# A scheduler's rank with a margin for small products: one term and one earliest time in a list-scheduled feed-forward kernel

## The chip, the cores and the metric

The kernel runs on one core of a Trainium2 chip. The metric is the time of one execution in microseconds (us). Before the change four executions took 459.94, 460.02, 460.11 and 460.18 us, median 460.06 us. The profile page was taken from one execution of 459.97 us.

## The reference

The input x is 64 samples of 64 channels by 1024 time steps. Each sample has a condition number, which picks a 64x64 matrix. The channels are mixed with it, and the result passes a linear layer with a gated low-rank addition (8 experts of rank 16, the best two of each token weighted by a softmax). The input is added at the end.

```python
W = weights[condition]                                   # 64 of 16 matrices, 64x64
h = jnp.einsum('bct,bcd->bdt', x, W)                     # condition mixing
gate_logits = jnp.einsum('bsd,ed->bse', h, gate_w)
weights, selected = jax.lax.top_k(gate_logits, 2)        # softmax over the two
result = jnp.einsum('bsd,od->bso', h, base_w) + base_b
low = jnp.einsum('bsd,erd->ebsr', h, lora_A)
lora_out = jnp.einsum('ebsr,eor,bse->bso', low, lora_B, w_full)
return x + result + 2.0 * lora_out
```

All is float32. The order of the two linear steps can be exchanged, and the kernel does that: it multiplies x by the wide weights first and applies the condition matrix to the product.

## The kernel before

**Tiling.** Tokens go in 32 tiles of 128 (two samples each). The weights of low-rank part, gate and base layer are put side by side and cut into three column blocks of 384, 388 and 388 columns; the 1024 inputs are cut into four pairs of 128. To keep float32 accuracy each operand is split into a high part (a rounded copy, made by ScalarE or VectorE, names `xh`, `wh_...`, `zh`, `bdh`, `lth`) and a low part (the difference, made by VectorE, names `xl`, `wl_...`, `zl`, `bdl`, `ltl`). Every product is then three matmuls: high by high, high by low, low by high (`zstep`, L407).

**Stages.** The first two pairs of tiles (`PLAIN`) are multiplied plainly while the weights arrive and are split. The other 14 pairs use a scheme with fewer products: sums of x blocks (`sum_x`, L292) and sums of weight blocks (`mix_w`, L342) are multiplied in a fixed order (`HEAD`, `TAIL`, `FINAL`), and the products are added and subtracted on VectorE into `st` buffers (`mix`, L740). A finished column block (`chunk`) is split (`split_z`) and goes to `post`.

**Small products.** `post` applies the condition matrix: `sums` (L434, matmuls on L447) multiplies `zh`, `zl` with `bdh`, `bdl`, and later adds the low-rank part with `lth`, `ltl`; `gate` works on the gate's logits; `tr` (L497, matmul on L500) transposes the weighted low-rank part. These steps of TensorE are marked `first=True`, except in the last two tiles. The big products are chained by the name `"order"`, so they keep their order; the small ones may stand anywhere between them.

**Condition matrices.** `load_cond` (L391) gathers one 128x128 matrix by an indirect DMA of GpSimd into `bdr`, casts it on ScalarE to `bdh` and subtracts on VectorE to `bdl`. There are two buffers. The first two loads stand at L597 and L598.

**The order of the work** is made at build time. `Program.add` records steps, each with its engines and the planner's assumed costs, what it reads and writes, and a due time. `Program.run` (L111) then lists them. It first goes backwards and gives each step a rank `late`: the latest start that keeps all due times, by the assumed costs. Then it goes forwards: it takes the engine that can start soonest, and on it, of the steps that are ready by then, one marked `first` if there is one, else the one of the smallest `late`. A step marked `first` is only offered `MARGIN` (1.2) after its inputs, so that on the chip it should not have to wait. `after=` gives a step an earliest time in the planner's own clock, and `early=True` keeps a step from being listed more than `AHEAD` (10) before its `late`. What comes out is a fixed order of instructions for TensorE, VectorE, ScalarE, GpSimd and the DMA queue of SyncE; on the chip an engine's instructions run in that order, each waiting for its inputs.

```python
for i in reversed(range(n)):
    s = steps[i]
    c, e = min(s["eng"].values()), next(iter(s["eng"]))
    late[i] = min([s["due"] - c] + [late[j] - hop(e, next(iter(steps[j]["eng"]))) - s["lag"] - c
                                    for j in succ[i]])
...
i, r = min(((i, r) for i, r in cand[e] if (max(r, port) if steps[i]["port"] else r) <= t + 1e-9),
           key=lambda q: (not steps[q[0]]["first"], late[q[0]], q[0]))
```

Of the kernel before, what the change touches and what calls it, by code (L numbers as in the profile page):

```python
# [41 lines left out]
PE, ACT, DVE, POOL, SP = "PE", "ACT", "DVE", "POOL", "SP"  # L42
# [4 lines left out]
ISSUE = 0.45  # L47
FLIGHT, DMA = 2.0, 1 / 360e3
QUEUE = 3.0
FIRST = 11.0  # L50
TWICE = 2.5
AHEAD = 10.0
MARGIN = 1.2
# [26 lines left out]
class Program:  # L80
# [7 lines left out]
    def add(self, engine, cost, fn, reads=(), writes=(), due=None, first=False, size=0.0, early=None, port=False,  # L88
            after=0.0):

        n = len(self.steps)
        engine, cost = (e if isinstance(e, (list, tuple)) else [e] for e in (engine, cost))
        deps = set()
        for b in list(reads) + list(writes):
            if b in self.writer:
                deps.add(self.writer[b])
        for b in writes:
            deps.update(self.readers.get(b, ()))  # L100
        for b in reads:
            self.readers.setdefault(b, []).append(n)
        for b in writes:
            self.writer[b], self.readers[b] = n, []
        deps.discard(n)
        self.steps.append(dict(eng=dict(zip(engine, cost)), fn=fn, deps=deps, first=first, size=size, port=port,
                               lag=FLIGHT + QUEUE + size * DMA if size else 0.0, after=after,
                               due=self.horizon if due is None else due,
                               early=SP in engine and not reads if early is None else early))

    def run(self):  # L111
        steps, n = self.steps, len(self.steps)
        succ = [[] for _ in steps]
        for i, s in enumerate(steps):
            for d in s["deps"]:
                succ[d].append(i)
        hop = lambda a, b: SAME[a] if a == b else HOP[a]
        late = [0.0] * n
        for i in reversed(range(n)):
            s = steps[i]  # L120
            c, e = min(s["eng"].values()), next(iter(s["eng"]))
            late[i] = min([s["due"] - c] + [late[j] - hop(e, next(iter(steps[j]["eng"]))) - s["lag"] - c
                                            for j in succ[i]])
        left = [len(s["deps"]) for s in steps]
        ready, end, by = [0.0] * n, [0.0] * n, [None] * n
        free = dict(START)
        cand = {e: set() for e in HOP}

        def offer(i):
            for e in steps[i]["eng"]:  # L130
                t = max([steps[i]["after"]] + [end[d] + hop(by[d], e) for d in steps[i]["deps"]])
                if steps[i]["early"]:
                    t = max(t, late[i] - AHEAD)
                t += MARGIN if steps[i]["first"] else 0.0
                cand[e].add((i, t))

        for i in range(n):
            if not left[i]:
                offer(i)
        done, port, wire = 0, 0.0, 0.0  # L140
        while done < n:
            best = None
            for e, c in cand.items():
                if c:
                    t = max(free[e], min(max(r, port) if steps[i]["port"] else r for i, r in c))
                    if best is None or t < best[0]:
                        best = (t, e)
            t, e = best
            i, r = min(((i, r) for i, r in cand[e] if (max(r, port) if steps[i]["port"] else r) <= t + 1e-9),
                       key=lambda q: (not steps[q[0]]["first"], late[q[0]], q[0]))  # L150
            for f in steps[i]["eng"]:
                cand[f] = {q for q in cand[f] if q[0] != i}
            end[i], by[i] = t + steps[i]["eng"][e], e
            free[e] = end[i]
            if steps[i]["size"]:
                end[i] = wire = max(end[i] + FLIGHT, wire) + steps[i]["size"] * DMA
            if steps[i]["port"]:
                port = end[i]
            steps[i]["fn"](e)
            done += 1  # L160
            for j in succ[i]:
                left[j] -= 1
                if not left[j]:
                    offer(j)
        return max(end)
# [3 lines left out]
def cond_ffn_kernel(ctx, tc, xT, x, idx, cw, wall, bias, lb, out):  # L169
# [22 lines left out]
    eng = {ACT: nc.scalar, DVE: nc.vector, POOL: nc.gpsimd}  # L192
# [3 lines left out]
    def many(n, shape, dt, name):  # L196
        return [sb.tile(shape, dt, name=f"{name}{j}") for j in range(n)]
# [8 lines left out]
    bdr, bdh, bdl = many(2, [P, P], F32, "bdr"), many(2, [P, P], F32R, "bdh"), many(2, [P, P], F32R, "bdl")  # L206
# [21 lines left out]
    add = pr.add  # L228

    def sub(e, o, a, b):  # L230
        eng[e].tensor_tensor(o, a, b.bitcast(F32), ALU.subtract)  # L231

    def copy(e, o, a):
        (nc.scalar.copy if e == ACT else nc.vector.tensor_copy)(o, a)  # L234
# [7 lines left out]
    def tt_cost(n):  # L242
        return 0.08 + 0.00104 * n
# [94 lines left out]
    def mix_w(o, a, b, f, over):  # L338
# [3 lines left out]
        add(DVE, tt_cost(2 * W), lambda e: nc.vector.tensor_tensor(r.ap(), x.ap(), y.ap(), f),  # L342
            [k for z in (x, y) if z is not r for k in z.keys], r.keys, port=True, after=FIRST)

# [46 lines left out]
    def load_cond(i):  # L391

        j = i % 2
        add(POOL, 1.04, lambda e: nc.gpsimd.indirect_dma_start(  # L394
            out=bdr[j], out_offset=None, in_=cw,
            in_offset=bass.IndirectOffsetOnAxis(ap=rows[:, i:i + 1], axis=0)),
            ["rows"], [("bdr", j)], size=4.0 * P * P, early=True)
        add(ACT, 0.28, lambda e: copy(e, bdh[j], bdr[j]), [("bdr", j)], [("bdh", j)])
        add(DVE, 0.25, lambda e: sub(e, bdl[j], bdr[j], bdh[j]), [("bdr", j), ("bdh", j)], [("bdl", j)], port=True)


    due = {}
# [192 lines left out]
    add(POOL, 1.1, make_rows, writes=["rows"])  # L595
    add(POOL, 0.6, lambda e: make_identity(nc, ident), writes=["ident"])
    load_cond(0)  # L597
    load_cond(1)  # L598
    for k in LASTK:
        load_split_w(f"b{k + 1}3")  # L600
# [11 lines left out]
    def plain(i, c, k):  # L612
        if (i, k) not in xa0:
            us = xrs.two()
            for d in range(2):
                load_x(i, k + d, us[d])
            xa0[i, k], xa0[i, k + 1] = split_x(us)
            xrs.give(*us)
        if (i, c) not in zb:
            zb[i, c] = f"z{take('z', 4)}"  # L620
            if c == 0 and i > 1:
                load_cond(i)
        ks, m = LASTK if c == 2 and i < 2 else range(KQ), f"b{k + 1}{c + 1}"
        for f in range(2):
            zstep(("plain", i, c, k, f), zb[i, c], xa0[i, k], SINGLE.get(m, m), f, k == ks[0] and f == 0,
                  k == ks[-1] and f == 1, CN[c])
        left[i, k] -= 1
        if not left[i, k]:
            xas.give(xa0[i, k])
        if k == ks[-1]:  # L630
            post(i, c, split_z(CN[c], lambda: bank[zb[i, c]][:, :CN[c]], zb[i, c]))
            if c == 2:
                late_sum(i)
                store(i, range(3))
# [229 lines left out]
```

## Time and profile before

| what | value |
|---|---|
| median of four executions | 460.06 us |
| the profiled execution | 459.97 us |
| its span, first to last instruction | 458.2 us |
| TensorE clock granted, mean | 0.998 |
| VectorE busy | 383.6 us (84%) |
| ScalarE busy | 227.4 us (50%) |
| GpSimd busy | 90.3 us (20%) |
| first product of x starts | 5.16 us |
| last matmul starts | 453.57 us |
| x loads (SyncE's queue) | 128 of 128 KB, median 2.9 us to landing |
| bias loads that add to what is there (GpSimd's queue) | 32 of 512 KB, median 6.4 us |
| stores (GpSimd's queue) | 30 of 512 KB, median 3.1 us |

The span is what lies between the first and the last instruction; the execution's own time has 1.8 us around it. "PE" is TensorE's matmul, "PEld" its weight load, DVE is VectorE, ACT ScalarE, POOL GpSimd and SP SyncE; a q behind a name is the engine's instruction queue, where DMAs are issued. A line of the timeline gives the start, the duration, engine, source line, operation, output and inputs, shapes, and in brackets how long the engine had been idle and what ended that.

### The profile page before, as it was taken

Reading aid. Unit: us, or ns where it says so; the run is one execution under the profiler, and the core shown is the slowest. Engines: PE = TensorE matmul, PEld = TensorE weight load, DVE = VectorE, ACT = ScalarE, POOL = GpSimd, SP = SyncE. Lnnn points to the kernel's source line nnn. Section 1 sums busy time; section 2 is a strip of 40 time slices with the busy share of each in tenths; the row PEclk is TensorE's granted clock in tenths of the full one; section 3 lists DMA queues with packets and bytes.
Section 4 is the critical chain, followed back from the end, with each engine's and each line's share of the span. In section 5 each row is a group of like instructions: output and inputs, shape, how many; then the busy total and the mean of one; then the engine's idle time right before and its main releaser. Section 6 shows DMA issues by size and latency. Waiting matters only on the chain.

```text
span 458.2 us, 7577 instructions
## 1 busy us (share of the span) xinstructions
PE 452.6 (99%) x2621; PEld 450.2 (98%) x2621; DVE 383.6 (84%) x941; ACT 227.4 (50%) x520; POOL 90.3 (20%) x107
## 2 busy tenths in 40 slices
PE   9999999999999999999999999999999999999996
PEld 8999999999999999999999999999999999999996
DVE  5999997878989788796987979799797988888674
ACT  5864666543736345373543646355354544546231
POOL 3020215121303021210303003030210403103000
PEclk9999999999999999999999999999999999999999
DMA  8932748975767453764847356555655746456152
GB/s 284 345 123 48 156 132 183 210 232 168 180 213 196 172 162 92 207 137 164 205 129 202 99 185 147 170 161 132 200 116 182 178 128 195 115 176 147 48 137 92
DMA packets 36229, 75.00 MB, mean 164 GB/s; under 512 B 4432, under 2 KB 22240, under 8 KB 36192
## 3 DMA queue, kind: packets, MB, share of 16 engines
q0 software_dynamic: 10560, 36.72, 32.9%
q1 hardware_dynamic: 25200, 37.32, 24.9%
q10 hardware_dynamic: 432, 0.49, 0.3%
q8 instruction: 20, 0.33, 0.3%
q14 instruction: 17, 0.14, 0.1%
HBM read 57.74 MB, written 16.78 MB: 163 GB/s over the span
## 4 chain that ended last, share of the span: by engine, by line
PE 99%; DVE 0%; issue 0%
PE ps_z L414 76%; PE ps_o L447 15%; PE ps_a L447 6%; PE ps_o L225 1%; PE ps_a L500 1%; DVE xtok L457 0%; DVE st L740 0%; PE ps_z L447 0%; DVE ltl L218 0%; DVE low L221 0%; DVE warm L311 0%
## 5 line engine op out<-in xcount | busy, mean ns | idle before, releaser
L231 DVE TENSOR_TENSOR xl<-xr,xh 128x512 fp32r<-128x512 f32 (+1 forms) x138 | 92.2, 671 | 20.8 <-ACT xh L234 20.7
L414 PE MATMUL ps_z<-wh_t_p,xh 128*128 128x388 f32 (+1 forms) x308 | 105.5, 342 | 0.1
L414 PE MATMUL ps_z<-wl_t_p,xh 128*128 128x388 f32 (+1 forms) x308 | 104.4, 339 | 0.0
L414 PE MATMUL ps_z<-wh_t_p,xl 128*128 128x388 f32 (+1 forms) x308 | 104.4, 339 | 0.0
L234 ACT CAST xh<-xr 128x512 fp32r<-128x512 f32 (+1 forms) x136 | 82.5, 610 | 37.5 <-PE ps_z L414 32.8
L740 DVE TENSOR_TENSOR st<-ps_z,st 128x388 f32<-128x388 f32 x126 | 70.3, 559 | 21.1 <-PE ps_z L414 20.1
L292 DVE TENSOR_TENSOR xr<-xr 128x256 f32<-128x256 f32 (+1 forms) x139 | 69.7, 527 | 2.2 <-DMA xr<-in_xT 1.8
L414 PE MATMUL ps_z<-wh_b_p,xh 128*128 128x388 f32 (+1 forms) x180 | 61.5, 341 | 0.0
L414 PE MATMUL ps_z<-wh_b_p,xl 128*128 128x388 f32 (+1 forms) x180 | 60.9, 338 | 0.0
L414 PE MATMUL ps_z<-wl_b_p,xh 128*128 128x388 f32 (+1 forms) x180 | 60.9, 338 | 0.0
L414 PEld LDWEIGHTS ps_z<-wh_t_p,xh 128*128 128x128 f32 x308 | 57.9, 188 | 1.2 <-DVE st L740 0.7
L414 PEld LDWEIGHTS ps_z<-wl_t_p,xh 128*128 128x128 f32 x308 | 57.9, 188 | 0.0
L414 PEld LDWEIGHTS ps_z<-wh_t_p,xl 128*128 128x128 f32 x308 | 57.9, 188 | 0.0
L464 POOL DMA_DIRECT2D out<-xtok x30 | 16.8, 560 | 192.3 <-DVE xtok L457 90.5
L234 ACT CAST zh<-st 128x388 fp32r<-128x388 f32 (+1 forms) x70 | 36.1, 517 | 22.0 <-DVE st L740 15.4
L381 POOL DMA_DIRECT2D xtok<-in_bias x28 | 27.4, 980 | 97.8 <-DMA xtok<-in_x 90.7
L394 POOL DMA_INDIRECT bdr<-in_cw,rows x32 | 37.6, 1175 | 27.6 <-DVE zl L231 17.5
L723 ACT ACTIVATE ps_z<-ps_z 128x388 f32<-128x388 f32 x42 | 20.1, 478 | 41.0 <-PE ps_z L414 39.0
L457 DVE TENSOR_TENSOR xtok<-ps_o,xtok 128x388 f32<-128x388 f32 (+1 forms) x56 | 30.9, 555 | 11.1 <-PE ps_o L447 10.7
L231 DVE TENSOR_TENSOR zl<-st,zh 128x388 fp32r<-128x388 f32 (+1 forms) x70 | 38.8, 555 | 0.9 <-ACT zh L234 0.6
L414 PEld LDWEIGHTS ps_z<-wh_b_p,xh 128*128 128x128 f32 x180 | 33.8, 188 | 0.2
L414 PEld LDWEIGHTS ps_z<-wl_b_p,xh 128*128 128x128 f32 x180 | 33.9, 188 | 0.0
(143 smaller groups left out, 875.5 us busy)
## 6 DMA issues: line engine op xcount, KB each, us to landing
xr<-in_xT SPq DMA_DIRECT2D x128, 128.0 KB, 2.9
xtok<-in_bias POOLq DMA_DIRECT2D x32, 512.0 KB, 6.4
out<-xtok POOLq DMA_DIRECT2D x30, 512.0 KB, 3.1
xtok<-in_x SPq DMA_DIRECT2D x28, 512.0 KB, 3.5
w_b<-in_w SPq DMA_DIRECT2D x10, 388.0 KB, 6.0
xtok<-in_x POOLq DMA_DIRECT2D x4, 512.0 KB, 5.3
out<-xtok SPq DMA_DIRECT2D x3, 194.0 KB, 2.2
bdr<-in_cw,rows POOLq DMA_INDIRECT x32, 4.7
```

Of the source, the lines that this page charges most:

```text
L225: nc.tensor.matmul(bank["o1"][:, :P], wz, wz, start=True, stop=True)
L231: eng[e].tensor_tensor(o, a, b.bitcast(F32), ALU.subtract)
L234: (nc.scalar.copy if e == ACT else nc.vector.tensor_copy)(o, a)
L292: add(DVE, tt_cost(2 * P * len(os)), lambda e: nc.vector.tensor_tensor(some(xr, os), some(xr, xs), some(xr, ys), f), [("xr", u) for u in s ...
L381: add(POOL, 1.1, lambda e: nc.gpsimd.dma_start(xtok[j], bias.broadcast_to([P, T]), accum_op=ALU.add), writes=keys, size=TWICE * 4.0 * T * P)
L394: add(POOL, 1.04, lambda e: nc.gpsimd.indirect_dma_start(out=bdr[j], out_offset=None, in_=cw, in_offset=bass.IndirectOffsetOnAxis(ap=rows[ ...
L414: nc.tensor.matmul(z, l[:, j, n], w.ap()[:, f, :cols], start=(start and q == 0), stop=(stop and q == 2), skip_group_check=True)
L447: nc.tensor.matmul(d, l, r, start=(start and m == 0), stop=(stop and m == len(mms) - 1), skip_group_check=True)
L457: add(DVE, 0.09 + 0.00104 * (s.stop - s.start), lambda e: nc.vector.tensor_tensor(xtok[j][:, o], bank[b][:, s], xtok[j][:, o], ALU.add), [ ...
L464: add(POOL, 1.0, lambda e: nc.gpsimd.dma_start(out[i * P:(i + 1) * P, o], xtok[j][:, o]), src, size=4.0 * P * (o.stop - o.start))
L723: add(ACT, 0.2 + 0.00085 * W, lambda e: nc.scalar.mul(z[b], z[x], scale), [BANKS[x]], [BANKS[b]])
L740: add(DVE, 0.09 + 0.00104 * W, lambda e: nc.vector.tensor_tensor(unit(u), a(), b(), f), reads, [ukey(u)])
```

## The change

Two edits.

- In the backward pass the rank of a step that feeds a step marked `first` becomes `MARGIN` smaller. The forward pass, which offers a marked step `MARGIN` after its inputs, is as before. As a rank is handed backwards from step to step, a step from which a path leads through several small products gets the margin several times.
- The cast of a condition matrix (`bdh`, on ScalarE) is not listed before 16.0 of the planner's clock (`CONDS`). Only the casts of the first two matrices can be touched by this.

No instruction is added or taken away: the same steps are listed in another order on all five queues.

```diff
@@ -47,6 +47,7 @@
 FLIGHT, DMA = 2.0, 1 / 360e3
 QUEUE = 3.0
+CONDS = 16.0
 FIRST = 11.0
@@ -119,7 +120,7 @@
             c, e = min(s["eng"].values()), next(iter(s["eng"]))
-            late[i] = min([s["due"] - c] + [late[j] - hop(e, next(iter(steps[j]["eng"]))) - s["lag"] - c
+            late[i] = min([s["due"] - c] + [late[j] - MARGIN * steps[j]["first"] - hop(e, next(iter(steps[j]["eng"]))) - s["lag"] - c
                                             for j in succ[i]])
@@ -395,7 +396,7 @@
             ["rows"], [("bdr", j)], size=4.0 * P * P, early=True)
-        add(ACT, 0.28, lambda e: copy(e, bdh[j], bdr[j]), [("bdr", j)], [("bdh", j)])
+        add(ACT, 0.28, lambda e: copy(e, bdh[j], bdr[j]), [("bdr", j)], [("bdh", j)], after=CONDS)
         add(DVE, 0.25, lambda e: sub(e, bdl[j], bdr[j], bdh[j]), [("bdr", j), ("bdh", j)], [("bdl", j)], port=True)
```

## The prediction, made before the changed kernel was run

> **What bounds the kernel now.** I read the page's busy shares and its chain first, then the waits of TensorE's weight loads, then busy time by stretch, then the timeline wherever TensorE waits.
>
> ```profile
> PE 452.6 (99%) x2621; PEld 450.2 (98%) x2621; DVE 383.6 (84%) x941; ACT 227.4 (50%) x520; POOL 90.3 (20%) x107
> ...
> PEclk9999999999999999999999999999999999999999
> ```
>
> ```profile
> PEld ps_z L414 <- DVE st L740: 0.7, 2, 0.4
> PEld ps_z L414 <- DVE xl L231: 0.3, 1, 0.3
> PEld ps_z L414 <- DVE wl_b_b L231: 0.2, 1, 0.2
> ```
>
> ```profile
> 16.00:32.00 16.00, 16.00 (x91) 15.82 (x91) 15.79 (x30) 10.98 (x21) 2.44 (x2) 1.00 0.63 216
> 32.00:48.00 16.00, 16.00 (x96) 15.93 (x95) 15.78 (x30) 8.80 (x20) 1.63 (x2) 1.00 0.24 51
> 48.00:64.00 16.00, 16.00 (x95) 15.97 (x94) 14.88 (x37) 10.62 (x24) 3.12 (x5) 1.00 0.68 152
> ```
>
> TensorE is the bound: 452.6 of 458.2 us, and 16.00 of 16.00 in every stretch from 16 to 432 us. The second fence holds all it waits for once the first product has started: four waits, 1.2 us, at 439.9 and 446.1 (0.7 together), 11.5 (0.3) and 26.8 (0.2). In the third the columns after the length are PE, PEld, DVE: from 16 to 48 us VectorE has 0.2 us to spare in 16, in both stretches. So a new order can save little, and what it can lose is decided where VectorE is full or where TensorE already waits. Of these places one lies inside the changed order, 26.8:
>
> ```profile
> 12.75 0.33 SPq L602 DMA_DIRECT2D xtok<-in_lb  x1
> 13.79 7.47 SPq L276 DMA_DIRECT2D xr<-in_xT  x8
> 21.39 0.35 SPq L326 DMA_DIRECT2D w_b<-in_w  x1
> ...
> 24.90 0.84 ACT L234 CAST wh_b_b<-w_b 128x776 fp32r<-128x776 f32 x1 [1.21 <-DMA w_b<-in_w]
> ...
> 25.23 0.55 DVE L231 TENSOR_TENSOR zl<-ps_z,zh 128x388 fp32r<-128x388 f32 x1
> ...
> 25.77 0.97 DVE L231 TENSOR_TENSOR wl_b_b<-w_b,wh_b_b 128x776 fp32r<-128x776 f32 x1
> ...
> 26.07 0.33 PE L447 MATMUL ps_a<-zh,bdh 128*128 128x384 f32 x1
> ...
> 26.60 0.34 PE L414 MATMUL ps_z<-wh_b_b,xh 128*128 128x388 f32 x1
> ...
> 26.79 0.19 PEld L414 LDWEIGHTS ps_z<-wl_b_b,xh 128*128 128x128 f32 x1 [0.18 <-DVE wl_b_b L231]
> 26.80 0.44 PE L414 MATMUL ps_z<-wl_b_b,xh 128*128 128x388 f32 x1
> ...
> 27.08 0.34 PE L414 MATMUL ps_z<-wh_b_b,xl 128*128 128x388 f32 x1
> ```
>
> The reader is to see a chain: the last weight block lands (24.9), is cast (to 25.74), its low half is made (to 26.74), and a product needs that half at once. While it is made, TensorE does a small product of three matmuls, L447 at 26.07, 26.25 and 26.42.
>
> **The change part by part.** No instruction is added or removed, so matmuls, casts and DMAs cost what they cost; only places in queues move. I compared the two built orders queue by queue.
>
> *Start and end.* The orders agree for the first 15 of VectorE's steps and 17 of ScalarE's, and on TensorE up to 26.07 us; after 433 us no queue differs. So the 5.16 us before the first product, the wait at 11.5, the two waits of 0.7 us and the 4.6 us from the last matmul to the span's end stay: 0.
>
> *The cast of the condition matrix held back.* The first (ScalarE, 14.85, 0.29 us) goes behind a weight cast and an x cast, 1.24 us; its product stands at 26.07. The second goes from 23.38 to just after 16.2; its matrix was gathered at 7.87, and ScalarE idles 0.72 us there (row at 17.77), which covers 0.31. Cost 0; without the idle time 0.3 us on a weight cast (19.59 to 20.43) whose low half VectorE makes only at 22.80.
>
> *The small product at 26.07.* In the new order this triple stands behind the triple at 26.60, and VectorE's `wl_b_b` stands ahead of the `zl` at 25.23. Followed by the rows: the big triple's first matmul needs the cast, done at 25.74, and starts at 26.07. Its second needs `wl_b_b`. VectorE can't start that before the cast's end, so moving it ahead of `zl` gains nothing: it runs 25.77 to 26.74, while VectorE idles from the end of `bdl` (25.31), and `zl` follows after it. The second matmul starts at 26.80 as before, the third at 27.08, the next triple could start at 27.25. But the small triple is still to do, 3 x 0.175 = 0.53 us, where before it was done by then. TensorE is 0.53 us late from here, and nothing downstream has idle time to take it back. VectorE is some 0.5 us late too, in a full stretch; as TensorE is late by the same, the distance between them is kept.
>
> This hangs on the landing at 24.9. In SyncE's queue the 512 KB load of `in_lb` goes behind four of the eight x loads, still ahead of the weight, so the same bytes precede it. In the DMA view the `in_lb` load takes 8.2 us, so it lands at 20.95; from there to 24.88 come eight x loads of 128 KB and 388 KB of weights, 1.45 MB in 3.9 us or 368 GB/s, above the page's busiest slice (345). The wires set the landing, not the issue. Ends: if it lands 0.7 us or more sooner, wait and loss are gone and the present loss there goes with it (the third matmul stands at 27.08 where 26.95 was due): -0.13. If it lands as now, +0.53; if as much later as the longest of the neighbouring waits of ScalarE on weights (0.72 at 17.77), +1.25. I take +0.53, for the bytes ahead are the same.
>
> *Everything else, 16 to 433 us.* Steps that feed small products go forward; `sum_x`, `mix_w`, weight splits and `mix` go back. The largest moves back are weight splits: the cast at 58.69 falls back by some 8 us, and its product comes over 30 us later. That is cover for 0. The tight ones are L740 instructions, which empty a bank the next product needs: behind most lie 0.2 to 0.3 us. Ten of them newly stand right behind a gate or transpose step (0.16 to 0.34 us by L489 and L493), seven no longer do. Ends for the net three: 0, if the step fits into the waits VectorE has there (21.1 us idle before L740 in all), and 0.3 each, 0.9. I take 0: before the L740 of the timeline that wait for TensorE VectorE was idle 0.2 to 0.8 us, more than such a step takes.
>
> Sum: 459.97 + 0.53 = **460.5 us**; the median of the runs shown is 0.09 above the profiled execution, which I leave in the range. The forecast's own range is 460.2 to 460.8.
>
> **The rivals.**
>
> *The weight lands sooner (chance 0.22).* For it: SyncE paced the eight x loads over 7.47 us, 0.93 each against 0.43 for an issue, so with smaller loads ahead the weight may be issued up to a microsecond earlier. Against it: the 368 GB/s. Time 459.97 - 0.13 = 459.8; with half of the gain 460.2.
>
> *Sums of x in front of their loads (0.21), the slow side.* The new order lists sums of x earlier in VectorE's queue, often ahead of an L740. Place:
>
> ```profile
> 187.43 0.56 DVE L740 TENSOR_TENSOR st<-ps_z,st 128x388 f32<-128x388 f32 x1 [1.89 <-PE ps_z L414]
> 187.91 1.02 DVE L292 TENSOR_TENSOR xr<-xr 128x512 f32<-128x512 f32 x2
> ```
>
> ```profile
> DMA to landing us min/median/max: 2.9/3.6/3.6
> ```
>
> The two sums now go ahead of the L740, into the 1.89 us in which VectorE was idle. They need x loads issued at 183.0 and 183.4, which take 3.6 us (second fence, the loads from 183.0 to 184.4) and land at 186.6 and 187.0; with TensorE 0.5 us late, at 187.1 to 187.5. The sums end at 188.5, and the L740 starts there rather than at 187.96: 0.5 late, and the next product that needs the bank stood 0.5 us behind its end. So the point from which it costs is 3.6 us of flight, and each further microsecond costs one. The nearest row for such a wait is 1.66 us (VectorE before its sum at 102.22). Between 0 and 1.66 I take 0.9: 461.4. Against it: most of the other sums moved forward go into idle time of VectorE with a microsecond or more behind the landing, and TensorE is seldom fed by VectorE in less than 0.7 us. By the Trainium skill ("TensorE: Matmul & The Clock Gate", Part 1) the clock falls to half after an idle window of about 3.4 us; by that rule a stall that long would cost more than itself. The granted clock stays at 1.00 across the idle 0.40 us at 439.9, so the sums above go by the stall alone, and no run here shows the longer case.
>
> *A gain that shows (0.05).* All waits but the start's are 1.2 us and 1.0 of them lie outside the changed order, so a gain over 0.2% (0.92 us) would need time that the page doesn't show as waiting: 458.9.
>
> **How the numbers follow.** Forecast 0.52, sooner landing 0.22, late sums 0.21, large gain 0.05. About 0.2% (0.92 us) is what a measurement of this kernel tells from no change: 459.14 to 460.98 is "same". Faster 0.05; slower 0.21, the late sums; same 0.74. The forecast by itself is a loss of 0.1%, inside that band. Range 459.6 to 461.6: down to the sooner landing, up past the late sums' price; outside are the large gain and stalls of over a microsecond.
>
> **What would show it.** Right: in the timeline of after, ps_a by L447 after the `wl_b_b` product at some 27.25, an idle of about 0.7 us before that weight load put down to `wl_b_b`, VectorE idle before `wl_b_b` behind ScalarE's cast, that cast still released by the DMA of the weight at 24.9, and the waits at 11.5, 440.4 and 446.7 as before. Wrong: the weight landing before 24.3 (first rival); weight loads waiting on L740 or `xl` between 100 and 430 us with VectorE waiting on x loads (second); a lower granted clock, or a first product that doesn't start near 5.2 us, neither of which any step here moves.

## The result, and the profile after

The changed kernel takes 460.93 us (median of 33 executions, 460.26 to 461.67), the kernel before, run beside it, 459.97 us (53 executions). The ratio is 1.002 with a 95% interval of 1.0015 to 1.0024: 0.96 us or 0.2% slower, inside the range given and 0.43 us above the predicted time.

The profiled execution took 461.4 us, half a microsecond more than the median, with a span of 459.3 us. First its page: the busy shares, and TensorE's weight loads in the list of waits (in us: total, times, longest). Lines of the kernel are one higher than before (L414 is L415, L740 is L741).

```profile
span 459.3 us, 7593 instructions
...
PE 453.1 (99%) x2621; PEld 450.0 (98%) x2621; DVE 383.8 (84%) x941; ACT 228.3 (50%) x520; POOL 90.3 (20%) x107
```

```profile
PEld ps_z L415 <- DVE st L741: 1.2, 3, 0.5
PEld ps_z L415 <- DVE wl_b_b L232: 0.6, 1, 0.6
PEld ps_z L415 <- DVE xl L232: 0.3, 1, 0.3
```

Busy times are as before. The waits have grown from 1.2 to 2.1 us: `wl_b_b` from 0.2 to 0.6, as forecast, and `st` by L741 from two waits (0.7) to three (1.2), which was not. The timeline shows both places. At 26 us:

```profile
24.81 0.84 ACT L235 CAST wh_b_b<-w_b 128x776 fp32r<-128x776 f32 x1 [1.07 <-DVE wl_e_p L232]
...
25.68 0.97 DVE L232 TENSOR_TENSOR wl_b_b<-w_b,wh_b_b 128x776 fp32r<-128x776 f32 x1 [0.31 <-ACT wh_b_b L235]
...
26.08 0.34 PE L415 MATMUL ps_z<-wh_b_b,xh 128*128 128x388 f32 x1
...
26.57 0.56 DVE L232 TENSOR_TENSOR zl<-ps_z,zh 128x388 fp32r<-128x388 f32 x1
26.70 0.19 PEld L415 LDWEIGHTS ps_z<-wl_b_b,xh 128*128 128x128 f32 x1 [0.61 <-DVE wl_b_b L232]
...
27.17 0.34 PE L448 MATMUL ps_a<-zh,bdh 128*128 128x384 f32 x1
```

The big triple starts at 26.08, its second matmul has to wait for `wl_b_b`, and the small triple that covered this wait comes behind it, at 27.17. Six matmuls that took 1.18 us before (26.07 to 27.25) take 1.62 (26.08 to 27.70): 0.44 us lost. (The page puts the cast's wait down to `wl_e_p`, which it does not read. In the DMA view its weight, issued at 20.50, takes 4.2 us and lands at 24.70.)

And at 417 us, where TensorE did not wait before:

```profile
413.51 0.42 DVE L293 TENSOR_TENSOR xr<-xr 128x256 f32<-128x256 f32 x1
...
414.62 1.29 DVE L293 TENSOR_TENSOR xr<-xr 128x512 f32<-128x512 f32 x2 [0.69 <-DVE xr L293]
...
415.83 0.55 DVE L232 TENSOR_TENSOR zl<-ps_z,zh 128x384 fp32r<-128x384 f32 x1
...
416.65 0.55 DVE L741 TENSOR_TENSOR st<-ps_z,st 128x388 f32<-128x388 f32 x1
...
417.25 0.19 PEld L415 LDWEIGHTS ps_z<-wh_h_p,xh 128*128 128x128 f32 x1 [0.47 <-DVE st L741]
```

Two sums of x stand in one row at 414.62. The first was there before too; it now waits for an x load that is issued at 410.47 and lands at 414.57 (before: 409.95 and 412.75). The second (0.6 us) is new. Behind them come `zl`, the gate's steps and L741, which ends at 417.20, and TensorE needs the bank that it empties. This costs 0.39 us. With the 0.44 at 26 us it makes up nearly all of the 0.88 us by which TensorE ends later than before (454.72 against 453.84).

The rest lies outside the span. In the median execution the time is 1.78 us longer than the span for the kernel before (1.73 to 1.86) and 2.04 for the changed one (mostly 1.93 to 2.14, but 1.75 to 1.80 in six executions). So of the 0.96 us between the medians 0.26 is outside the span and 0.7 inside.

### The profile page after: what moved, and what is told of

Read it like the earlier page. It is cut to its first block, busy times and chain, and to the rows that moved or that the text cites. A ratio compares the mean times of both kernels' runs of the same rounds, so it can differ in the third digit from the quotient of the medians.

```text
span 459.3 us, 7593 instructions
## 1 busy us (share of the span) xinstructions
PE 453.1 (99%) x2621; PEld 450.0 (98%) x2621; DVE 383.8 (84%) x941; ACT 228.3 (50%) x520; POOL 90.3 (20%) x107
## 4 chain that ended last, share of the span: by engine, by line
PE 91%; DVE 3%; DMA 3%; issue 1%; ACT 0%; SPq 0%; ACTq 0%; DVEq 0%
PE ps_z L415 70%; PE ps_o L448 15%; PE ps_a L448 6%; DMA w_b<-in_w 2%; PE ps_a L501 1%; DMA xr<-in_xT 1%; DVE wl_b_b L232 1%; DVE xl L232 1%; DVE wl_b_p L232 0%; DVE xr L293 0%; DVE st L741 0%; DVE w_b L343 0%; DVE zl L232 0%; DVE wl_e_p L232 0%; DVE w_e L343 0%
## 5 line engine op out<-in xcount | busy, mean ns | idle before, releaser
L232 DVE TENSOR_TENSOR xl<-xr,xh 128x512 fp32r<-128x512 f32 (+1 forms) x138 | 92.3, 671 | 21.4 <-ACT xh L235 21.3
L415 PE MATMUL ps_z<-wh_t_p,xh 128*128 128x388 f32 (+1 forms) x308 | 105.2, 342 | 0.1
L415 PE MATMUL ps_z<-wl_t_p,xh 128*128 128x388 f32 (+1 forms) x308 | 104.3, 339 | 0.0
L415 PE MATMUL ps_z<-wh_t_p,xl 128*128 128x388 f32 (+1 forms) x308 | 104.1, 338 | 0.0
L741 DVE TENSOR_TENSOR st<-ps_z,st 128x388 f32<-128x388 f32 x126 | 70.4, 559 | 19.5 <-PE ps_z L415 17.7
L415 PE MATMUL ps_z<-wh_b_p,xh 128*128 128x388 f32 (+1 forms) x180 | 61.5, 342 | 0.0
L415 PE MATMUL ps_z<-wh_b_p,xl 128*128 128x388 f32 (+1 forms) x180 | 60.8, 338 | 0.0
L415 PE MATMUL ps_z<-wl_b_p,xh 128*128 128x388 f32 (+1 forms) x180 | 60.8, 338 | 0.0
L415 PEld LDWEIGHTS ps_z<-wh_t_p,xh 128*128 128x128 f32 x308 | 57.9, 188 | 1.3 <-DVE st L741 0.7
L415 PEld LDWEIGHTS ps_z<-wh_t_p,xl 128*128 128x128 f32 x308 | 57.9, 188 | 0.0
L415 PEld LDWEIGHTS ps_z<-wl_t_p,xh 128*128 128x128 f32 x308 | 57.9, 188 | 0.0
L724 ACT ACTIVATE ps_z<-ps_z 128x388 f32<-128x388 f32 x42 | 20.1, 478 | 38.2 <-PE ps_z L415 35.8
L235 ACT CAST bdh<-bdr 128x128 fp32r<-128x128 f32 x32 | 9.5, 299 | 50.0 <-PE ps_o L448 50.0
L415 PEld LDWEIGHTS ps_z<-wh_b_p,xh 128*128 128x128 f32 x180 | 33.8, 188 | 0.3
```

The costliest lines, as they stand in the source:

```text
L415: nc.tensor.matmul(z, l[:, j, n], w.ap()[:, f, :cols], start=(start and q == 0), stop=(stop and q == 2), skip_group_check=True)
L724: add(ACT, 0.2 + 0.00085 * W, lambda e: nc.scalar.mul(z[b], z[x], scale), [BANKS[x]], [BANKS[b]])
L741: add(DVE, 0.09 + 0.00104 * W, lambda e: nc.vector.tensor_tensor(unit(u), a(), b(), f), reads, [ukey(u)])
```

## Where the second wait begins

Followed back through the queues, the new sum leads to 402 us. The kernel before, timeline of four engines:

```profile
401.30 0.34 PE L414 MATMUL ps_z<-wh_t_p,xh 128*128 128x388 f32 x1
...
402.01 0.48 ACT L723 ACTIVATE ps_z<-ps_z 128x388 f32<-128x388 f32 x1 [1.65 <-PE ps_z L414]
...
402.40 0.61 ACT L234 CAST xh<-xr 128x512 fp32r<-128x512 f32 x1
...
403.55 0.68 DVE L231 TENSOR_TENSOR xl<-xr,xh 128x512 fp32r<-128x512 f32 x1
...
404.14 0.30 ACT L234 CAST bdh<-bdr 128x128 fp32r<-128x128 f32 x1 [1.12 <-PE ps_o L447]
...
404.26 0.80 SPq L276 DMA_DIRECT2D xr<-in_xT  x2
...
407.69 1.15 DVE L292 TENSOR_TENSOR xr<-xr 128x256 f32<-128x256 f32 x2
```

The changed kernel at the same place:

```profile
404.13 0.30 ACT L235 CAST bdh<-bdr 128x128 fp32r<-128x128 f32 x1 [3.25 <-PE ps_o L448]
...
404.26 0.34 PE L415 MATMUL ps_z<-wh_t_p,xh 128*128 128x388 f32 x1
...
404.99 0.48 ACT L724 ACTIVATE ps_z<-ps_z 128x388 f32<-128x388 f32 x1 [0.57 <-PE ps_z L415]
...
405.38 0.61 ACT L235 CAST xh<-xr 128x512 fp32r<-128x512 f32 x1
...
406.06 0.69 DVE L232 TENSOR_TENSOR xl<-xr,xh 128x512 fp32r<-128x512 f32 x1
...
406.78 0.83 SPq L277 DMA_DIRECT2D xr<-in_xT  x2
```

The reader is to compare the starts. On TensorE a big triple that stood at 401.30, ahead of three small products, stands at 404.26 behind them. Only after it may ScalarE overwrite the `xh` buffers that it reads: the cast goes from 402.40 to 405.38. On ScalarE, too, the condition matrix's cast `bdh` now stands first, and ScalarE idles 3.25 us for the small products that free its buffer. The low half `xl` goes from 403.55 to 406.06, and only its end frees the x buffer into which SyncE loads: the two loads go from 404.26 to 406.78 and land at 409.28 and 409.65 in place of 406.51 and 407.51. The planner therefore lists their sums later, after 413 us, and one of them in front of L741. Everything that feeds small products moved forward, which is the change; what it pushed back here is the feed of a big one, 13 us on.

## The experiments

Most are the changed kernel or the kernel before with moves made in the finished list: `MOVES` holds pairs (step, step in front of which it is put), and no step is put ahead of what it depends on. The hook adds ten lines, so line numbers are ten higher than in the kernel it is put into. e5 and e6 take back one edit each and make no moves; e11 and e12 add instructions to GpSimd's list (e11 without the hook).

```diff
+        for m, at in MOVES:
+            k = next(k for k, q in enumerate(plan) if q[0] == m)
+            q = plan.pop(k)
+            plan.insert(next(k for k, r in enumerate(plan) if r[0] == at), q)
```

Steps named below: 135 the small triple on `ps_a` at 26 us, 185 the big one that needs `wl_b_b`; 95 `wl_b_b`, 170 `zl`; 93, 94 load and cast of that weight; 104, 105 load and cast of `lb`; 2221 the big triple, 2222 ScalarE's step on its bank (L724), 2262 the cast of x, 2263 its `xl`, 2200 `bdh`, all near 402 to 406 us; 2347, 2348 the two sums of x.

| kernel | median us | ratio to before (95%) | six matmuls at 26 us | lost at 412 to 418 |
|---|---|---|---|---|
| before | 459.97 | | 1.18 | 0 |
| changed | 460.93 | 1.0020 (1.0015 to 1.0024) | 1.62 | 0.4 |
| e1, 26 us undone | 460.61 | 1.0012 (1.0003 to 1.0021) | 1.15 | 0.3 |
| e2, 26 us alone, on before | 460.40 | 1.0005 (0.9996 to 1.0014) | 1.71 | 0 |
| e3, sums back | 461.06 | 1.0021 (1.0012 to 1.0030) | 1.67 | 0.7 |
| e4, e1 and e3 | 461.04 | 1.0018 (1.0009 to 1.0027) | 1.37 | 0.7 |
| e9, sum behind L741 | 460.71 | 1.0016 (1.0006 to 1.0025) | 1.31 | 0 |
| e10, 26 us and the chain undone | 460.29 | 1.0007 (0.9998 to 1.0016) | 1.23 | 0 |

The last two columns come from one profiled execution each: the time from the start of the first of the two triples to the start of what follows (1.06 without a wait), and the time by which matmul starts are late there. The ratios are to the kernel before on the same chip: 460.16 us beside e1 to e4, 459.99 beside e5, e9 and e10, 460.08 beside e8 and e11, 459.97 beside e12.

**The exchange at 26 us.** e1 takes it out of the changed kernel, e2 puts it into the one before.

```diff
+MOVES = ((135, 185), (170, 95), )    # e1
+MOVES = ((185, 135), (95, 170), )    # e2
```

> The changed kernel, but the first small product of TensorE (the triple on ps_a) and VectorE's zl stand again ahead of the big triple and of the low half wl_b_b that it needs. Theory (the loss at 26.7 us is this one exchange): the idle 0.61 us before the weight load of wl_b_b falls to 0.2, ps_a starts near 26.1, and 0.46 of the 0.96 us comes back: about 460.5 us (0.5 above the kernel before). The wait at 417 us stays near 0.4. Rival 1 (VectorE is full to 48 us, the stall is only where its backlog shows): the wait moves to a later weight load before 60 us and the time stays 460.9. Rival 2 (the wait at 417 us is set by a load with a time of its own): TensorE comes 0.46 sooner to 417 and waits 0.85 there, time 460.9.

> The kernel before, with only this exchange made in its list: the big triple that needs wl_b_b ahead of the triple on ps_a, and wl_b_b ahead of zl on VectorE. Theory: the exchange alone costs 0.46 to 0.53 us: about 460.5 us, TensorE idle some 0.65 us before the weight load of wl_b_b, no new wait at 415 us. Rival 1 (the rest of the new order is needed for the loss): within 0.1 us of the kernel before, 460.0. Rival 2 (any lateness at the start makes a later sum of x wait): 460.9, with a wait on L740 near 416 us too.

e1: the wait for `wl_b_b` is back to that of the kernel before, the wait at 417 is still there (0.3) and no longer than it was, and no new wait stands between 27 and 60 us. (Two waits for `wl_b_b` at 5.14 and 6.18, of 0.36 and 0.40 us, stand ahead of everything that the moves touch. One or both stand in nine of the profiles and in neither main one, and by 25 us e1's TensorE is level with the changed kernel's.) That is the theory; by the ratios, 1.0020 to 1.0012, some 0.4 us came back, though the intervals overlap. e2: 1.71 us for the six matmuls and no wait at 416, so the exchange alone makes this loss and does not bring the second. In time, 0.24 us above the kernel before with an interval that holds 0: the trace settles it, the time does not. The loss varies from one execution to the next, for TensorE and the weight's landing each shift by some tenths: over the profiles with the small triple first the six matmuls took 1.15 to 1.39 us, behind it 1.31 to 1.71, both with the weight's load where it was. So the order costs some 0.3 to 0.4 us on the mean of these profiles.

**The sums alone (a miss).**

```diff
+MOVES = ((2347, 2294), (2348, 2294), )                            # e3
+MOVES = ((135, 185), (170, 95), (2347, 2294), (2348, 2294), )     # e4
```

> The changed kernel, but the two sums of x that stood at 407.69 us before, and now stand (one of them right behind the sum that waits for an x load) ahead of the subtraction L741, go back to the head of that stretch of VectorE. Theory (the 0.39 us at 417.25 is the second sum's 0.6 us in front of L741): TensorE's wait at 417.25 is gone or under 0.1, time about 460.5 us (0.5 above before). Rival (the wait comes from the x load's late landing alone; the sum that needs it stands ahead of L741 anyway): the wait keeps 0.3 to 0.4 us, time 460.9.

> The changed kernel with both edits: the small product and zl ahead again, and the two sums of x at their old place. Everything else of the new order stays, some hundreds of moved steps. Theory (these two places are all that costs): 460.93 - 0.46 - 0.39 = 460.1 us, within 0.15 of the kernel before, TensorE's waits after its start 1.2 us in sum. Rival (the rest of the order costs on its own, in the tail of 0.2 us or in waits too small to see): 460.3 or more.

Neither came: 461.06 and 461.04 us, no gain. The wait at 417 is gone, and a larger one stands at 412. Timeline of e3:

```profile
409.49 1.15 DVE L303 TENSOR_TENSOR xr<-xr 128x256 f32<-128x256 f32 x2 [0.80 <-DMA xr<-in_xT]
410.56 0.68 DVE L242 TENSOR_TENSOR xl<-xr,xh 128x512 fp32r<-128x512 f32 x1
411.16 0.55 DVE L751 TENSOR_TENSOR st<-ps_z,st 128x388 f32<-128x388 f32 x1
...
412.84 0.19 PEld L425 LDWEIGHTS ps_z<-wh_t_p,xh 128*128 128x128 f32 x1 [0.73 <-DVE st L751]
```

At their old place the sums wait 0.80 us for the x loads, because these come 2.5 us later in the changed kernel. So the fall of the sums in the list follows from the late loads, and moving both back does not help; this is what led to the chain at 402 us.

**The sum behind L741, and the chain undone.**

```diff
+MOVES = ((2348, 2252), )                                          # e9
+MOVES = ((135, 185), (170, 95), (2221, 2176), (2222, 2200),       # e10
+         (2262, 2200), (2263, 2197), (2347, 2294), (2348, 2294), )
```

> The changed kernel with one step moved: the second sum of x (15.23 after 400, 0.6 us) goes from just ahead of zl, gate and L741 to just behind L741. The loads stay as late as they are. Theory (the price at 417.25 is this sum in front of L741): L741 stands some 0.6 us sooner, near 416.05, TensorE's wait at 417.25 is gone, 460.93 - 0.39 = 460.5 us. Rival 1 (the first sum, which waits for the x load issued at 410.47, is enough): the wait keeps 0.2 us or more. Rival 2 (the sum is needed soon): a new wait appears between 418 and 421 us and takes the gain.

> The changed kernel with the exchange at 26 us undone, and with the head of the chain near 402 us undone: the big triple that frees an x buffer goes back ahead of three small products of TensorE, the cast of x (L235) ahead of the cast of a condition matrix on ScalarE, its low half ahead of the output sums on VectorE, and the two sums of x back to the place they had before. All other moves of the new order stay. Theory (the chain starts there: triple, cast, low half, x load, sum, L741): the x loads issued at 406.8 are issued near 404.8, the sums find their x at 408, TensorE waits neither at 412 nor at 417, and the time is 460.1 us, within 0.15 of the kernel before. Rival 1 (the loads are late for another reason): issue stays near 406.4, the sums wait some 0.8 us and TensorE some 0.6 us at 412 as when the sums alone were moved, 461.0. Rival 2 (the rest of the order costs too): waits elsewhere, 460.4 or more.

e9, timeline: the sum that waits, L741 (here L751), then the second sum.

```profile
414.02 0.69 DVE L303 TENSOR_TENSOR xr<-xr 128x512 f32<-128x512 f32 x1 [0.53 <-DVE xr L303]
...
415.65 0.56 DVE L751 TENSOR_TENSOR st<-ps_z,st 128x388 f32<-128x388 f32 x1
416.13 0.68 DVE L303 TENSOR_TENSOR xr<-xr 128x512 f32<-128x512 f32 x1
```

TensorE waits neither at 417 nor after it until the two waits of the tail. The loads are as late as in the changed kernel (406.34), so the price was the second sum in front of L741; the first, for all its waiting, costs nothing. By the ratios, 1.0020 to 1.0016, this is worth 0.2 us, less than the 0.39 of the trace, and the intervals overlap.

e10, timeline and weight loads' waits:

```profile
402.56 0.61 ACT L245 CAST xh<-xr 128x512 fp32r<-128x512 f32 x1
...
403.70 0.68 DVE L242 TENSOR_TENSOR xl<-xr,xh 128x512 fp32r<-128x512 f32 x1
...
404.42 0.80 SPq L287 DMA_DIRECT2D xr<-in_xT  x2
...
408.17 1.14 DVE L303 TENSOR_TENSOR xr<-xr 128x256 f32<-128x256 f32 x2
```

```profile
PEld ps_z L425 <- DVE st L751: 0.7, 2, 0.4
```

With the triple, the cast and the low half back in place, the loads are issued at 404.42 and the sums at 408.17 no longer wait; only the two waits of the tail are left on L751, as before the change. The span is that of the kernel before (median 458.3 against 458.2), though hundreds of other moves remain: to within 0.1 us these two places are all that the new order costs within the span. e10 moves the triple, ScalarE's step, the cast, the low half and the sums together. So it shows that the chain starts in this group, and not which link comes first, TensorE's order or the place of `bdh` on ScalarE. The time, 460.29, is 0.3 above the kernel before, and 0.28 of that lies outside the span (2.06 against 1.78).

**The two edits one at a time.**

```diff
-CONDS = 16.0
+CONDS = 0.0                                                       # e5
```

```diff
-late[j] - MARGIN * steps[j]["first"] - hop(...)
+late[j] - hop(...)                                                # e6
```

> The margin in the rank alone, CONDS set to 0. The list then has the small product near 26 us six triples sooner, but the two casts of condition matrices 4 and 15 places sooner on ScalarE, between weight casts at 8.5 and 11.8 us. The chain at 402 to 417 us is as in the changed kernel. Theory (the loss at 26 needs both edits, that at 417 the margin alone): no loss at 26.7, the wait at 417 us stays at 0.3 to 0.4; the early casts cost 0 to 0.6 at 11 us, where a weight load already waits 0.3: 460.4 us without, 461.0 with 0.6. Rival (the margin makes both losses): 460.9 with a wait of 0.6 on wl_b_b at 26.7.

> The earliest time of the condition matrices' casts alone, the rank as before. The list differs from the kernel before in 3 places on ScalarE (the first cast goes behind a weight cast and an x cast) and nowhere else. Theory: 0, as the cast is needed at 26 us: 460.0 to 460.2 us, ps_a at 26.07, no wait at 417. Rival (its low half is made late and the small product waits): a wait of TensorE on bdl near 26 us, up to 0.5 us.

e6 took 460.04 us in one execution, with TensorE's order that of the kernel before: no change that shows, as expected. e5 took 464.60 us, 1.0104 (1.0088 to 1.0119), 4.6 us slower; the expectation named 0.6 at most. Timeline of e5:

```profile
12.67 0.30 ACT L245 CAST bdh<-bdr 128x128 fp32r<-128x128 f32 x1 [3.45 <-DMA bdr<-in_cw,rows]
12.88 0.83 ACT L245 CAST wh_b_b<-w_b 128x776 fp32r<-128x776 f32 x1
...
14.07 0.44 PE L425 MATMUL ps_z<-wh_b_b,xh 128*128 128x384 f32 x1 [2.79 <-ACT xh L245]
```

The cast stands on ScalarE ahead of the weight cast; its matrix, gathered by an indirect DMA issued at 6.51 beside the weight loads, takes some 6 us to land. ScalarE idles 3.45 us, and TensorE 2.79 behind it. I had costed the cast by its 0.3 us and not by what it waits for. So the second edit does nothing by itself that shows, and mends what the first does at the start. The wait near 417 stays in e5 (0.33 at 419.98), as expected: that loss is the first edit's. The exchange at 26 us needs both: with the margin alone the small triple stands six places ahead of the big one, in the kernel before one place ahead, with both edits one behind.

**When the weight lands.** e7 (on the changed kernel) and e8 (on the one before) put the weight's load ahead of the 512 KB of `lb`.

```diff
+MOVES = ((104, 56), (105, 152), )                                 # e7
+MOVES = ((104, 56), (105, 152), (95, 170), )                      # e8
```

> The changed kernel with the last weight's load ahead of the 512 KB load of in_lb and its cast ahead of lbh on ScalarE; the small product stays behind the big triple, and the chain at 402 to 417 us stays. Theory (the wires set the landing; the first loss is the wait for wl_b_b and nothing else): landing near 23.3 in place of 24.7, wl_b_b done by 26.3, no idle time before its weight load at 26.4, and 0.45 us less: 460.5 us, with the wait at 417 us of 0.2 to 0.4 left. Rival (the landing is set by the issue): cast still near 24.8, the wait at 26.7 us stays, 460.9.

> A candidate from the kernel before: the last weight's load goes ahead of the 512 KB load of in_lb on SyncE's queue, ScalarE casts it ahead of lbh, and VectorE makes wl_b_b ahead of zl. The small product stays where it was. Theory (the wires set when the weight lands, 368 GB/s): it lands 512 KB or 1.4 us sooner, near 23.4, is cast by 24.6, wl_b_b is done by 26.2, and the wait of 0.1 to 0.2 us at 26.8 is gone: 459.8 us, 0.1 to 0.2 under the kernel before, too little to be told apart in time, but plain in the timeline. Rival (the issue or ScalarE's queue sets it): cast still near 24.8, time unchanged or worse by what lbh then delays.

e7, timeline:

```profile
23.73 0.84 ACT L245 CAST wh_b_b<-w_b 128x776 fp32r<-128x776 f32 x1 [1.14 <-DMA w_b<-in_w]
...
25.08 0.95 DVE L242 TENSOR_TENSOR wl_b_b<-w_b,wh_b_b 128x776 fp32r<-128x776 f32 x1
...
26.09 0.19 PEld L425 LDWEIGHTS ps_z<-wl_b_b,xh 128*128 128x128 f32 x1 [0.22 <-DVE wl_b_b L242]
```

The cast starts 1.08 us sooner in e7 and 1.40 in e8, where 1.4 was worked out from 512 KB at 368 GB/s. The six matmuls take 1.22 and 1.06 us. The weight's load itself was also issued sooner, by 0.65 us in e7 (19.85 against 20.50) and 1.32 in e8 (20.07 against 21.39), so these two runs do not tell the bytes ahead of it from its own issue. e7 took 460.54 us in one execution with the wait at 417 left. e8 took 460.00 where 459.8 was named, with a ratio of 0.9990 to 1.0008: no gain over the kernel before that shows.

**The time outside the span, and a try at a faster kernel.** Nothing in the order explains 0.26 us outside the span, but the changed kernel has 12 more semaphore instructions on GpSimd. e11 adds 30 memsets of a small tile to the kernel before, e12 the tile and one memset to e8.

```diff
+    pad = sb.tile([P, 1], F32, name="pad")
...
+        if i > 1:                        # e12: if i == 2
+            nc.gpsimd.memset(pad, 0.0)
```

> The kernel before with 30 small memsets added on GpSimd, each behind the gather of a condition matrix; GpSimd is busy 20% and waits for none of them. The new lists have 1.78 us (kernel before) or 2.05 us (changed kernel) between the execution's time and its span, and the changed kernel has 12 more semaphore instructions on GpSimd. Theory (the time outside the span grows with the length of GpSimd's list): 0.27 x 30 / 12 = 0.7 more outside, 2.45 us, and 460.6 us in all. Rival (it is not the length of that list): 1.78 us outside, 460.0 us in all.

> The candidate with the last weight's load ahead of in_lb (460.0 us, no wait at 26.8), with the small tile that the 30 memsets wrote and one of these memsets, not 30. With the tile and 30 memsets the kernel before took 459.64 us in place of 460.08, and its casts of weights ran 0.3 us sooner from 7 us on. Theory (the tile, which moves the buffers behind it, is what helps): 459.6 us with the weight casts at 7.1, 8.9 and 10.3 us, and 0.1 less for the wait at 26.8 that is gone: 459.5. Rival 1 (the memsets themselves): 460.0. Rival 2 (chance of one lot of runs): 460.0, and single runs scattered from 459.8 to 460.3.

Outside the span e11 has 1.76 us: the length of GpSimd's list is not it. Where the 0.26 us come from stays open; they go with the list (medians of 1.74 to 1.81 for the kernel before and lists a few moves away from it, 2.01 to 2.09 for the changed one and those near it, 1.91 for e5). The traces show one thing that goes with them. In the profiles of the changed list and of all those near it, one packet of 8 KB, of the kind "instruction", starts some 1.8 us after the last instruction; in the profiles of the others, e5 among them, none does. Whether this packet makes the time longer is not shown. Unasked, e11 took 459.64 us (0.9981 to 1.0000) and e12 459.79 (0.9984 to 1.0003), the lowest medians of all. A weight cast that starts at 7.1 is no sign of the tile, for in the changed kernel, e4 and e7, which have none, it does so too. e11 and e12 beat the changed kernel clearly; against the kernel before the intervals reach 1, and whether the tile, which moves the buffers behind it, does this or chance is not settled.

## Why the prediction was right, and where it was not

*Start and end, 0.* Right in the order: first product at 5.16, waits at 11.5, 440.8 and 447.0 in size as before. But the sum added the span's changes to the execution's own time as though what lies around the span were fixed at 1.8 us. What lies around it became 2.04 in the median: 0.26 us that no term held. "No instruction is added" holds for the work; of semaphore instructions there are 16 more (7593 against 7577).

*The cast of the condition matrix, 0.* Right for the change as made: e6 shows no cost.

*The small product at 26.07, +0.53.* The mechanism is shown by e1, e2 and e7: small triple behind, VectorE idle before `wl_b_b` behind ScalarE's cast, ps_a at 27.17 where 27.25 was named. The landing came as forecast: the load was issued 0.9 us sooner (20.50 against 21.39) and landed 0.1 sooner (24.70 against 24.80). That full wires set it in both kernels is not shown. From issue to landing of the weight the wires moved 308 GB/s at a share of 0.99 in the changed kernel, but 241 GB/s at 0.76 in the kernel before, with 0.38 between 21.4 and 22.4. So that the landing hardly moved is in part luck: the earlier issue met fuller wires. The size was 0.44 in the profile, as `wl_b_b` started 0.09 sooner, and 0.2 (e2) to 0.4 (e1) by the ratios.

*Everything else, taken 0, ends to 0.9.* This step failed: 0.39 us in the profile, some 0.2 by the ratios (e9). It counted gate and transpose steps right ahead of L740, and priced sums only as going forward, ahead of their loads, though it notes that some go back. The sum at 415 fell back, into a row behind one that waits for its load. SyncE's two loads at 404.26 went back 2.5 us, which the order alone does not show, because their place in the queue is the same and only the release of the buffer came later.

*The rivals.* The weight landing sooner did not come as a rule, though one profile, that of e9, has it at 24.22. The sums of x in front of their loads: at 186 us, the place named, VectorE idles 0.25 us for its load and TensorE not at all. At 417 a sum stands ahead of L741 too, but it got there by falling back, and by e9 the price is its own 0.6 us and not the waiting for a load; the 0.39 is under half of the 0.9 taken. So this rival did not come true, though it named the right kind of step.

*The total.* 460.93 lies in the range given, which the rivals had made wide, but outside the 460.2 to 460.8 of the forecast's own mechanism. About 0.4 us came as forecast; the 0.2 to 0.4 at 417 and the 0.26 outside the span stood in no term. That the total came within 0.43 us is therefore in part luck.

## What to carry to other kernels

A scheduler that brings forward what feeds one kind of work pushes back what stands beside it: follow each pushed step to the buffer that it frees, to the load into that buffer and to the consumer of that load, over all the queues, for the loss may stand 13 us further on. In a queue of fixed order a moved step costs what it waits for and not what it takes: a cast of 0.3 us held ScalarE for 3.45. Where moving a late consumer back to its old place does not help, its input is late, and the cause lies further up.

## What the runs showed of the hardware that was not expected

Issuing a load 0.9 us sooner brought its landing 0.1 us forward, and from issue to landing the wires were busy to 0.99, where they had been busy to 0.76. Issuing it 0.65 to 1.3 us sooner with 512 KB taken out from ahead of it brought the cast 1.1 to 1.4 us forward. Three indirect gathers of a 128x128 matrix beside the weight loads took 5.4 to 6.1 us to land in e5. And the time between an execution's length and its span was 1.78 us for one order of the same work and 2.04 for the other, without a cause that these runs could name. It was 1.77 to 1.80 for the kernel before on four chips, and 2.01 to 2.09 for lists near the changed one on three of them.

TensorE's idle 2.79 us in e5 left its granted clock at 1.00 in the stretches after it, and matmuls followed each other by 0.175 us as before. The Trainium skill ("TensorE: Matmul & The Clock Gate", Part 1) puts the loss of the clock at an idle window of about 3.4 us; this wait stays under it and agrees, and no run here shows a longer one.
